# First layer's epilogue: the norm of u from a quadratic form per row, h + y from g and the neighbour sums

## The chip, the cores and the metric

The kernel runs on one core of a Trainium2 chip. The metric is the device time of one execution in microseconds (us). Before the change its median over eight runs is 2209.0 us (2207.34 to 2211.43).

A core has five engines with instruction queues of their own: PE (TensorE, matrix products), DVE (VectorE), ACT (ScalarE), POOL (GpSimd) and SP (SyncE, which here only issues transfers). Each queue is worked off in order; between queues there are semaphores. A tile has 128 partitions.

## What is computed

The reference is four graph layers over 4096 nodes with 128 features and a dense 0/1 adjacency matrix of 4096 x 4096, each followed by a residual sum and a layer norm. Only the first layer matters here. It works in hyperbolic space (c = 1), row by row after one sum over neighbours:

```python
h = proj(mobius_add(proj(mobius_matvec(weight, x)), hyp_bias))
x_tangent = logmap0(h)
x_local = jax.vmap(lambda xi: logmap(xi, h))(h)              # all pairs of rows
adj_att = adj * jax.nn.sigmoid(logits)
support_t = jnp.einsum('ij,ijd->id', adj_att, x_local)       # u, one row per node
h_agg = proj(expmap(h, support_t))                           # tanh(lambda |u| / 2) u / |u|, then mobius_add with h
out = proj(expmap0(proj_tan0(h_agg)))
x = layernorm(x + out)
```

`expmap(h, u)` needs |u| per row, then the Moebius sum of h and a multiple of u, then the norm of that sum; the outer maps need one more norm. So the rows are run over several times, with a few operations on one number per row between the passes.

## The kernel before

All features are float32 in SBUF as 32 row tiles of 128 rows by 128 features, `NT = 32`; a *column* is a 128 x 32 tile that holds one number per row.

The first part of `layer0` builds g = h / (1 - |h|^2) in `H` (the first 128 columns of `HA`), its transpose `HT`, its squared norms `gg`, and columns such as `b`, `bhalf` (b/2), `b2x` (2b), `rb`. Then `pair_loop` runs over the 36 pairs of blocks of 512 rows in an order written out by hand (`PAIR_ORDER`, under a manual schedule). For each pair PE turns the adjacency blocks and forms dot products, ACT and DVE make the weights, and PE sums g over the neighbours (`sum_i` L675, `sum_j` L690); DVE adds the sums up in `XA` (`add_up`, L704). `X` is its first 128 columns: v, the weighted sum of g over the neighbours; its last column is the same sum over the extra column of `HA`.

Behind that stands the epilogue, which is not hand-ordered: the framework's scheduler sets the order of each queue by itself, and buffers come from pools with a fixed count.

- L453 loads x once more into the memory of `HT` (`x0`), a transfer on SP's queue.
- L459: POOL writes `Hb` = b * g, 32 tiles.
- L462 and L465: for each tile DVE takes the dot product of g and v (`gv`), and ACT scales v by b/2 in place.
- L466 to L468: the column `sm`.
- `combine` (L470 to L481) is called in three loops. It puts `src * a + add` into `X` on DVE (L475, one operation per tile) and takes the sum of its squares, on DVE (L477) for some tiles and on ACT (L481) for the others. On both engines such a sum is two instructions: the operation and the read of the accumulator. The calls are
  - L485: u = sm * g + (b/2) v, with |u|^2 into `uu`;
  - L492: w = sg * u + Hb, with |w|^2 into `wsq`;
  - L508: c2 * w + c1 * Hb, with its square into `gsq`.
- Between the first two calls `un` (L488, a square root) and `th` (a tanh) are made on ACT, each with a load of its function table (L239), and `sg` on DVE. Between the last two, `den`, `rden`, `c2`, `c1` (L493 to L501), and then L504 and L506 scale `Hb` by `c1`, odd tiles on POOL, even ones on ACT.
- The rest makes `gf` from `gsq`, and L520 forms x0 + gf * w tile by tile, followed by the layer norm of four tiles at a time (`normalise_tile`).

The second layer begins with transposes of `X` on PE, products with its weights, and transfers of the results (`qk`).

Of the kernel before, what the change touches and what calls it, by code (L numbers as in the profile page):

```python
# [9 lines left out]
F32 = mybir.dt.float32  # L10
F32R = mybir.dt.float32r
AF = mybir.ActivationFunctionType
ALU = mybir.AluOpType
# [3 lines left out]
P = 128  # L17
EPS_LN = 1e-5
MIN_NORM = 1e-15
# [23 lines left out]
class Net:  # L43
# [234 lines left out]
    def layer0(self, x, weight, bias, att_w, att_b):  # L278
        nc, tc, N, NT, D = self.nc, self.tc, self.N, self.NT, self.D
        W1 = min(1024, N)  # L280
        WH = min(1024, N)
        X = self.X
        with ExitStack() as ctx:
# [12 lines left out]
            H = HA[:, :, 0:D]  # L296
# [14 lines left out]
            junk = self.wide.tile([P, 4, P], F32, tag="wt", name="wt")  # L311
# [90 lines left out]
            b = self.ts("b", hsq, -1.0, ALU.mult, 1.0, ALU.add)  # L402
            nc.vector.tensor_scalar(b, b, MIN_NORM, None, op0=ALU.max)
            rb = self.rec("rb", b)
            ga, gb = self.tt("ga", ca, rb, ALU.mult), self.tt("gb", cb, rb, ALU.mult)
            de = self.cols.tile([P, 2, NT], F32, tag="de", name="de")
            gg = self.col("gg")
            for g in self.groups():
                p = self.ps_t.tile([P, 4, P], F32, tag="pt", name="pt")
                for k, t in enumerate(g):  # L410
                    c = slice(t, t + 1)
                    junk = pre.tile([P, P], F32, tag="junk", name="junk", bufs=4)
# [28 lines left out]
            b2x, bhalf = self.ts("b2x", b, 2.0, ALU.mult), self.ts("bhalf", b, 0.5, ALU.mult)  # L441
# [7 lines left out]
            self.pair_loop(HT, HA, dr, ex, rows, adp, early)  # L449


            x0 = HT.rearrange("p (t d) -> p t d", d=D)
            nc.sync.dma_start(out=x0, in_=self.rows(x))  # L453
            late = ctx.enter_context(tc.tile_pool(name="late0", bufs=1))
            rot = ctx.enter_context(tc.tile_pool(name="rot0", bufs=4))
            Hb = late.tile([P, NT, D], F32, tag="Hb", name="Hb")
            gv = self.col("gv")
            for t in range(NT):
                nc.gpsimd.tensor_scalar(Hb[:, t, :], H[:, t, :], b[:, t : t + 1], None, op0=ALU.mult)  # L459
            for t in range(NT):  # L460
                junk = rot.tile([P, P], F32, tag="junk", name="junk")
                nc.vector.scalar_tensor_tensor(  # L462
                    junk, H[:, t, :], 1.0, X[:, t, :], op0=ALU.mult, op1=ALU.mult, accum_out=gv[:, t : t + 1]
                )
                nc.scalar.activation(X[:, t, :], X[:, t, :], AF.Copy, scale=bhalf[:, t : t + 1])  # L465
            sm = self.tt("sm", gv, b2x, ALU.mult)  # L466
            nc.vector.tensor_tensor(sm, sm, self.XA[:, :, D], ALU.subtract)
            nc.vector.tensor_tensor(sm, sm, bhalf, ALU.mult)  # L468

            def combine(t, a, src, add, sq, of_eight):  # L470

                k = slice(t, t + 1)
                junk = rot.tile([P, P], F32, tag="junk", name="junk")
                x = X[:, t, :]
                nc.vector.scalar_tensor_tensor(x, src[:, t, :], a[:, k], add[:, t, :], op0=ALU.mult, op1=ALU.add)  # L475
                if t * of_eight % 8 < of_eight:
                    nc.vector.scalar_tensor_tensor(  # L477
                        junk, x, 1.0, x, op0=ALU.mult, op1=ALU.mult, accum_out=sq[:, k]
                    )
                else:  # L480
                    nc.scalar.activation(junk, x, AF.Square, accum_out=sq[:, k])  # L481

            uu, wsq, gsq = self.col("uu"), self.col("wsq"), self.col("gsq")
            for t in range(NT):
                combine(t, sm, H, X, uu, 2)  # L485


            un = self.norm("un", uu)  # L488
            th = self.act("sg", self.tt("unb", un, rb, ALU.mult), AF.Tanh)
            sg = self.tt("sgu", th, self.rec("run", un), ALU.mult)  # L490
            for t in range(NT):
                combine(t, sg, X, Hb, wsq, 2)  # L492
            den = self.ts("den2", th, -1.0, ALU.mult, 1.0, ALU.add)  # L493
            nc.vector.tensor_scalar(th, th, 1.0, None, op0=ALU.add)
            nc.vector.tensor_tensor(den, den, th, ALU.mult)
# [3 lines left out]
            rden = self.rec("rden2", den)  # L499
            c2 = self.tt("c2", rden, b, ALU.mult)  # L500
            c1 = self.tt("c1", rden, wsq, ALU.mult)  # L501
            for t in range(NT):
                if t % 2:
                    nc.gpsimd.tensor_scalar(Hb[:, t, :], Hb[:, t, :], c1[:, t : t + 1], None, op0=ALU.mult)  # L504
                else:
                    nc.scalar.activation(Hb[:, t, :], Hb[:, t, :], AF.Copy, scale=c1[:, t : t + 1])  # L506
            for t in range(NT):
                combine(t, c2, X, Hb, gsq, 3)  # L508

            gn = self.norm("gn", gsq)  # L510
            gf = self.to_ball("gp", gn)
            gn = self.tt("gn2", gn, gf, ALU.mult)
            nc.vector.tensor_scalar(gn, gn, MIN_NORM, None, op0=ALU.max)
            th = self.act("gth", gn, AF.Tanh)
# [3 lines left out]
            nc.vector.tensor_tensor(gf, gf, self.to_ball("gp2", th), ALU.mult)  # L518
            for t in range(NT):
                nc.vector.scalar_tensor_tensor(  # L520
                    X[:, t, :], X[:, t, :], gf[:, t : t + 1], x0[:, t, :], op0=ALU.mult, op1=ALU.add
                )
                if t % 4 == 3:
                    self.normalise_tile(t // 4, on_scalar=True)
# [1029 lines left out]
```

## Time and profile before

| what | value |
|---|---|
| median of 8 runs | 2209.0 us |
| lowest, highest | 2207.34, 2211.43 us |
| the profiled execution's own time | 2209.21 us |
| its span, first to last instruction | 2207.3 us |
| PE, DVE, ACT, POOL busy in the span | 88%, 85%, 67%, 4% |
| last neighbour sum on PE ends (start of the epilogue) | 766.5 us after the span's start |
| first tile of the last loop (L520) starts | 819.9 us |
| granted PE clock, mean | 0.953 of full speed |

How to read it: the profile gives, for each engine, when an instruction started and how long it was in the engine. Two instructions that follow each other on an engine overlap a little, so the distance of their starts is shorter than the duration of one. A "group" is all instructions of one line and shape, with their mean duration and the idle time of the engine just ahead of them; "<-" names what ended that idle time. The chain of waits is the sequence of work that ended last, followed back from the end of the span.

### The profile page before, as it was taken

To read this page: it belongs to the slowest core of one execution; us is meant where nothing else is said; L and a number is where in the kernel's file an instruction comes from. 1 tells how busy PE (TensorE), PEld (TensorE's weight loads), DVE (VectorE), ACT (ScalarE), POOL (GpSimd) and SP (SyncE) were. 2 spreads that over 40 slices of the span, in tenths; PEclk is the share of its full clock that TensorE was granted. 3 is DMA by queue.
4 is the path that set the end of the run, shared out by engine and by line. 5 is a ranking of instruction groups with operands and counts; after the bars stand their busy time and mean duration, and the time that the engine had idled before them with its cause. 6 is when DMAs were issued, how large, how long until landed. Compare 5 with 4: busy or idle time off the path is not lost.

```text
span 2207.3 us, 24053 instructions
## 1 busy us (share of the span) xinstructions
PE 1945.0 (88%) x8720; PEld 1050.4 (48%) x8720; DVE 1880.9 (85%) x2732; ACT 1476.5 (67%) x1858; POOL 98.1 (4%) x146
## 2 busy tenths in 40 slices
PE   4588888888888708999999999999997999989998
PEld 4376667676666505433333333333333444434443
DVE  6799999999999887789999999999898345458887
ACT  5799999999999774687777787877883212210000
POOL 2000000000000322210000000000000000000000
PEclk7789999999999956999999999999999999999999
DMA  3467565667666307885646465565455777667883
GB/s 93 139 207 242 201 220 203 239 210 244 209 210 213 116 1 247 212 228 173 200 163 188 172 200 180 174 191 175 168 195 229 284 280 272 253 224 270 292 299 111
DMA packets 112868, 448.44 MB, mean 203 GB/s; under 512 B 9760, under 2 KB 20064, under 8 KB 71776
## 3 DMA queue, kind: packets, MB, share of 16 engines
q1 hardware_dynamic: 94160, 361.82, 46.7%
q10 hardware_dynamic: 9360, 68.16, 9.1%
q0 software_dynamic: 9216, 16.78, 4.2%
q8 instruction: 73, 1.20, 0.2%
q14 instruction: 59, 0.48, 0.1%
HBM read 369.10 MB, written 77.63 MB: 202 GB/s over the span
## 4 chain that ended last, share of the span: by engine, by line
PE 40%; DVE 33%; ACT 19%; issue 5%; DMA 3%; SPq 0%; POOL 0%; ACTq 0%; DVEq 0%; POOLq 0%
PE pv L926 10%; PE pa L1260 10%; PE pa L1437 9%; DVE e L909 9%; PE ps L900 6%; ACT e L907 4%; ACT w L612 3%; DVE w L620 3%; DVE nat L890 2%; DVE t L603 2%; DVE t L648 2%; DMA adjT<-at 2%; DVE w L652 2%; ACT at L584 2%; ACT y L627 2%
## 5 line engine op out<-in xcount | busy, mean ns | idle before, releaser
L909 DVE SCALAR_TENSOR_TENSOR e<-at,e 128x2048 f32<-128x2048 f32 x256 | 583.1, 2288 | 69.5 <-ACT e L907 68.9
L907 ACT ACTIVATE e<-ps 128x1024 f32<-128x1024 f32 x512 | 493.6, 1025 | 145.4 <-PE ps L900 125.6
L926 PE MATMUL pv<-e,VA 128*64 128x512 f32 x2048 | 495.8, 605 | 6.9 <-DVE e L909 6.3
L900 PE MATMUL ps<-QS,KS 128*128 128x512 f32 x1024 | 312.7, 424 | 5.3 <-ACT e L907 3.0
L900 PEld LDWEIGHTS ps<-QS,KS 128*128 128x128 f32 x1024 | 171.5, 189 | 230.4 <-ACT e L907 175.3
L926 PEld LDWEIGHTS pv<-e,VA 128*64 128x64 f32 x2048 | 124.7, 136 | 248.8 <-issue 214.6
L1260 PE MATMUL pa<-ring,Y 128*128 128x512 f32 x512 | 227.1, 597 | 0.0
L580 PE MATMUL ptA<-ident,ad 128*128 128x128 f32 x1024 | 158.8, 283 | 59.4 <-ACT at L584 49.5
L1437 PE MATMUL pa<-w,F 128*128 128x512 f32 x448 | 197.0, 598 | 0.0
L580 PEld LDWEIGHTS ptA<-ident,ad 128*128 128x128 f32 x1024 | 120.5, 144 | 139.7 <-ACT at L584 95.3
L1434 DVE SCALAR_TENSOR_TENSOR w<-rho,col,ring 128x512 f32<-128x512 f32 x224 | 162.9, 749 | 25.6 <-PE pa L1437 13.3
L596 PE MATMUL pz<-HT 128*128 128x512 f32 x288 | 154.5, 640 | 21.3 <-DVE w L663 14.2
L675 PE MATMUL pi<-HA,w 128*128 128x129 f32 x1152 | 156.2, 281 | 0.6 <-DVE w L652 0.6
L1260 PEld LDWEIGHTS pa<-ring,Y 128*128 128x128 f32 x512 | 96.7, 193 | 112.8 <-issue 111.9
L620 DVE TENSOR_TENSOR w<-w,at 128x2048 f32<-128x2048 f32 x64 | 146.4, 2287 | 0.5 <-ACT at L584 0.5
L675 PEld LDWEIGHTS pi<-HA,w 128*128 128x128 f32 x1152 | 143.9, 197 | 3.6 <-issue 2.3
L1437 PEld LDWEIGHTS pa<-w,F 128*128 128x128 f32 x448 | 84.3, 191 | 107.2 <-issue 80.0
L881 ACT ACTIVATE nat<-nat 128x2048 f32<-128x2048 f32 x64 | 122.6, 1916 | 4.0 <-DMA nat<-in_adj_dram 4.0
L690 PE MATMUL pj<-HA,w 128*128 128x129 f32 x896 | 109.5, 274 | 3.0 <-DVE w L663 3.0
L603 DVE SCALAR_TENSOR_TENSOR t<-ei,de,pz 128x512 f32<-128x512 f32 x144 | 104.1, 745 | 6.7 <-DMA ei<-rows 6.6
L690 PEld LDWEIGHTS pj<-HA,w 128*128 128x128 f32 x896 | 104.6, 191 | 3.2 <-DVE w L663 3.2
L658 PE MATMUL ptz<-ident,t 128*128 128x128 f32 x448 | 69.0, 281 | 30.0 <-DVE w L663 22.5
(359 smaller groups left out, 2461.8 us busy)
## 6 DMA issues: line engine op xcount, KB each, us to landing
ring<-adjT SPq DMA_DIRECT2D x128, 1024.0 KB, 5.4
ad<-in_adj_dram SPq DMA_DIRECT2D x64, 1024.0 KB, 5.4
adjT<-at SPq DMA_DIRECT2D x64, 1024.0 KB, 4.9
nat<-in_adj_dram ACTq DMA_DIRECT2D x64, 1024.0 KB, 5.0
at<-adjT SPq DMA_DIRECT2D x63, 1024.0 KB, 4.8
qk<-cut SPq DMA_DIRECT2D x16, 512.0 KB, 11.8
KS<-qk POOLq DMA_DIRECT2D x32, 256.0 KB, 7.5
QS<-qk POOLq DMA_DIRECT2D x32, 256.0 KB, 5.8
```

What stands on the lines that cost most here:

```text
L580: nc.tensor.transpose(pt[:, ib, :], ad[:, ib, jb * P : (jb + 1) * P], self.ident)
L596: nc.tensor.matmul(pz, lhsT=HT[:, j * P : (j + 1) * P], rhs=HT[:, I * S : (I + 1) * S], start=True, stop=True)
L620: nc.vector.tensor_tensor(w, w, st[p][f"at{k}"], ALU.mult)
L675: nc.tensor.matmul(row[I, "po"][ib // 2][:, ib % 2, :], lhsT=st[p]["w0"][:, jb, ib * P : (ib + 1) * P], rhs=HA[:, 4 * J + jb, :], start=False,
L690: nc.tensor.matmul(pj[:, a, :], lhsT=st[p]["w1"][:, ib, jb * P : (jb + 1) * P], rhs=HA[:, 4 * I + ib, :], start=(ib == 0), stop=(ib == 3),)
L900: nc.tensor.matmul(p[:, h, :], lhsT=KS[:, h2 + h, jb * P : (jb + 1) * P], rhs=QS[I % 2][:, h2 + h, :], start=True, stop=True,)
L907: nc.scalar.activation(e[:, h2 : h2 + 2, :], p, AF.Exp)
L909: nc.vector.scalar_tensor_tensor(e, at[:, jb % 4, :].unsqueeze(1).to_broadcast([P, NH, S]), 0.0, e, op0=ALU.not_equal, op1=ALU.mult,)
L926: nc.tensor.matmul(st["po"][h // 2][g : g + 64, :], lhsT=VA[:, o : o + 64], rhs=e[:, h, :], start=(jb == 0), stop=(jb == NT - 1), skip_gro ...
L1260: nc.tensor.matmul(st["pa"], lhsT=Y[:, 4 * J + jb, :], rhs=at[:, jb, :], start=False, stop=(J == NS - 1 and jb == 3), skip_group_check=True,)
L1434: nc.vector.scalar_tensor_tensor(w, rho[:, I * S : (I + 1) * S], col[:, 0, j : j + 1], at[:, jb, :], op0=ALU.max, op1=ALU.mult)
L1437: nc.tensor.matmul(pa, lhsT=F[:, j, :], rhs=w, start=False, stop=(j == NT - 1), skip_group_check=True)
```

## The change

u is no longer formed. With u = sm * g + (b/2) v its squared norm is sm^2 |g|^2 + 2 sm (b/2) g.v + (b/2)^2 |v|^2, so the first loop takes |v|^2 (`vv`, on ACT) instead of scaling v, and `quadratic` works on columns alone. `Hb` goes too: w is formed as wg * g + wv * v with wg = sg * sm + b and wv = sg * b/2, and the last combination as c2 * w + (c1 * b) g. For each of these two, `scaled` puts the second product into a buffer `part` (tiles 1, 4 and 6 of every eight on POOL, the others on ACT), and DVE adds the first. The results are kept in a tile of their own, `w`, and the pool of rotating buffers has 6 of each kind instead of 4. Three of four squares are on ACT in both loops. In the changed file the dot product is L480, the square of v L484, `scaled` L473 and L475, the combinations L499 and L523, the squares L502, L506, L526 and L530.

```diff
--- before.py
+++ after.py
@@ -449,47 +449,61 @@
             self.pair_loop(HT, HA, dr, ex, rows, adp, early)
 
 
+
             x0 = HT.rearrange("p (t d) -> p t d", d=D)
             nc.sync.dma_start(out=x0, in_=self.rows(x))
             late = ctx.enter_context(tc.tile_pool(name="late0", bufs=1))
-            rot = ctx.enter_context(tc.tile_pool(name="rot0", bufs=4))
-            Hb = late.tile([P, NT, D], F32, tag="Hb", name="Hb")
-            gv = self.col("gv")
+            rot = ctx.enter_context(tc.tile_pool(name="rot0", bufs=6))
+            w = late.tile([P, NT, D], F32, tag="w", name="w")
+            gv, vv, wsq = self.col("gv"), self.col("vv"), self.col("wsq")
+
+            def quadratic(name, a, c):
+
+                q, r = self.tt(name, a, gg, ALU.mult), self.tt(name + "r", c, gv, ALU.mult)
+                nc.vector.scalar_tensor_tensor(q, r, 2.0, q, op0=ALU.mult, op1=ALU.add)
+                nc.vector.tensor_tensor(q, q, a, ALU.mult)
+                nc.vector.tensor_tensor(r, c, c, ALU.mult)
+                nc.vector.tensor_tensor(r, r, vv, ALU.mult)
+                nc.vector.tensor_tensor(q, q, r, ALU.add)
+                nc.vector.tensor_scalar(q, q, MIN_NORM * MIN_NORM, None, op0=ALU.max)
+                return q
+
+            def scaled(t, dst, src, factor):
+                if t % 8 in (1, 4, 6):
+                    nc.gpsimd.tensor_scalar(dst, src, factor, None, op0=ALU.mult)
+                else:
+                    nc.scalar.activation(dst, src, AF.Copy, scale=factor)
+
             for t in range(NT):
-                nc.gpsimd.tensor_scalar(Hb[:, t, :], H[:, t, :], b[:, t : t + 1], None, op0=ALU.mult)
-            for t in range(NT):
+                k = slice(t, t + 1)
                 junk = rot.tile([P, P], F32, tag="junk", name="junk")
                 nc.vector.scalar_tensor_tensor(
-                    junk, H[:, t, :], 1.0, X[:, t, :], op0=ALU.mult, op1=ALU.mult, accum_out=gv[:, t : t + 1]
+                    junk, H[:, t, :], 1.0, X[:, t, :], op0=ALU.mult, op1=ALU.mult, accum_out=gv[:, k]
                 )
-                nc.scalar.activation(X[:, t, :], X[:, t, :], AF.Copy, scale=bhalf[:, t : t + 1])
+                junk = rot.tile([P, P], F32, tag="junk", name="junk")
+                nc.scalar.activation(junk, X[:, t, :], AF.Square, accum_out=vv[:, k])
             sm = self.tt("sm", gv, b2x, ALU.mult)
             nc.vector.tensor_tensor(sm, sm, self.XA[:, :, D], ALU.subtract)
             nc.vector.tensor_tensor(sm, sm, bhalf, ALU.mult)
 
-            def combine(t, a, src, add, sq, of_eight):
-
-                k = slice(t, t + 1)
-                junk = rot.tile([P, P], F32, tag="junk", name="junk")
-                x = X[:, t, :]
-                nc.vector.scalar_tensor_tensor(x, src[:, t, :], a[:, k], add[:, t, :], op0=ALU.mult, op1=ALU.add)
-                if t * of_eight % 8 < of_eight:
-                    nc.vector.scalar_tensor_tensor(
-                        junk, x, 1.0, x, op0=ALU.mult, op1=ALU.mult, accum_out=sq[:, k]
-                    )
-                else:
-                    nc.scalar.activation(junk, x, AF.Square, accum_out=sq[:, k])
-
-            uu, wsq, gsq = self.col("uu"), self.col("wsq"), self.col("gsq")
-            for t in range(NT):
-                combine(t, sm, H, X, uu, 2)
-
-
-            un = self.norm("un", uu)
+
+            un = self.norm("un", quadratic("uu", sm, bhalf))
             th = self.act("sg", self.tt("unb", un, rb, ALU.mult), AF.Tanh)
             sg = self.tt("sgu", th, self.rec("run", un), ALU.mult)
+            wg, wv = self.tt("wg", sg, sm, ALU.mult), self.tt("wv", sg, bhalf, ALU.mult)
+            nc.vector.tensor_tensor(wg, wg, b, ALU.add)
             for t in range(NT):
-                combine(t, sg, X, Hb, wsq, 2)
+                k = slice(t, t + 1)
+                part = rot.tile([P, P], F32, tag="part", name="part")
+                scaled(t, part, X[:, t, :], wv[:, k])
+                nc.vector.scalar_tensor_tensor(w[:, t, :], H[:, t, :], wg[:, k], part, op0=ALU.mult, op1=ALU.add)
+                junk = rot.tile([P, P], F32, tag="junk", name="junk")
+                if t % 4 == 3:
+                    nc.vector.scalar_tensor_tensor(
+                        junk, w[:, t, :], 1.0, w[:, t, :], op0=ALU.mult, op1=ALU.mult, accum_out=wsq[:, k]
+                    )
+                else:
+                    nc.scalar.activation(junk, w[:, t, :], AF.Square, accum_out=wsq[:, k])
             den = self.ts("den2", th, -1.0, ALU.mult, 1.0, ALU.add)
             nc.vector.tensor_scalar(th, th, 1.0, None, op0=ALU.add)
             nc.vector.tensor_tensor(den, den, th, ALU.mult)
@@ -499,13 +513,21 @@
             rden = self.rec("rden2", den)
             c2 = self.tt("c2", rden, b, ALU.mult)
             c1 = self.tt("c1", rden, wsq, ALU.mult)
+            nc.vector.tensor_tensor(c1, c1, b, ALU.mult)
+
+            gsq = self.col("gsq")
             for t in range(NT):
-                if t % 2:
-                    nc.gpsimd.tensor_scalar(Hb[:, t, :], Hb[:, t, :], c1[:, t : t + 1], None, op0=ALU.mult)
+                k = slice(t, t + 1)
+                part = rot.tile([P, P], F32, tag="part", name="part")
+                scaled(t, part, H[:, t, :], c1[:, k])
+                nc.vector.scalar_tensor_tensor(w[:, t, :], w[:, t, :], c2[:, k], part, op0=ALU.mult, op1=ALU.add)
+                junk = rot.tile([P, P], F32, tag="junk", name="junk")
+                if t % 4 == 3:
+                    nc.vector.scalar_tensor_tensor(
+                        junk, w[:, t, :], 1.0, w[:, t, :], op0=ALU.mult, op1=ALU.mult, accum_out=gsq[:, k]
+                    )
                 else:
-                    nc.scalar.activation(Hb[:, t, :], Hb[:, t, :], AF.Copy, scale=c1[:, t : t + 1])
-            for t in range(NT):
-                combine(t, c2, X, Hb, gsq, 3)
+                    nc.scalar.activation(junk, w[:, t, :], AF.Square, accum_out=gsq[:, k])
 
             gn = self.norm("gn", gsq)
             gf = self.to_ball("gp", gn)
@@ -518,7 +540,7 @@
             nc.vector.tensor_tensor(gf, gf, self.to_ball("gp2", th), ALU.mult)
             for t in range(NT):
                 nc.vector.scalar_tensor_tensor(
-                    X[:, t, :], X[:, t, :], gf[:, t : t + 1], x0[:, t, :], op0=ALU.mult, op1=ALU.add
+                    X[:, t, :], w[:, t, :], gf[:, t : t + 1], x0[:, t, :], op0=ALU.mult, op1=ALU.add
                 )
                 if t % 4 == 3:
                     self.normalise_tile(t // 4, on_scalar=True)
```

## The prediction

> **What bounds the kernel now.** The change touches only the epilogue of the first layer, so I first cut the span into stages (busy time of each engine in each stretch). The page's overall shares (PE 88%, DVE 85%) say nothing here: in these 50 us PE does nothing.
>
> ```profile
> core 0: us, PE busy (x) PEld busy (x) DVE busy (x) ACT busy (x) POOL busy (x), PEclk, DMA share, GB/s
> ...
> 767.20:775.90 8.70, 0.00 (x0) 0.00 (x0) 8.48 (x69) 8.36 (x29) 8.70 (x13) 0.61 0.00 1
> 775.90:786.70 10.80, 0.00 (x0) 0.00 (x0) 10.25 (x48) 9.18 (x53) 1.18 (x7) 0.50 0.00 0
> 786.70:790.10 3.40, 0.00 (x0) 0.00 (x0) 0.94 (x6) 3.02 (x4) 0.00 (x0) 0.50 0.01 2
> 790.10:800.90 10.80, 0.00 (x0) 0.00 (x0) 10.65 (x51) 8.81 (x48) 0.00 (x0) 0.50 0.00 0
> 800.90:802.10 1.20, 0.00 (x0) 0.00 (x0) 1.02 (x5) 0.00 (x0) 0.00 (x0) 0.50 0.00 0
> 802.10:815.40 13.30, 0.00 (x0) 0.00 (x0) 12.32 (x56) 11.32 (x56) 10.64 (x16) 0.50 0.00 1
> ```
>
> The reader sees no PE work and no transfers (last column 0 to 2 GB/s): nothing but DVE, ACT and POOL passing 32 row tiles to each other, with a barrier of small column operations between loops. I name the loops A (767.2, g·v and scaling of X), B (775.9, u and |u|²), C (790.1, w and |w|²) and D (802.1, scaling of Hb, then the combination and its norm). Whatever is saved in one is saved in the span, because the next barrier waits for the last tile. The chain of waits confirms it: it stays in these loops, and the table loads and column operations stand between them.
>
> ```profile
> 786.69 1.28 ACT L239
> 787.99 0.23 ACT un L239
> 788.24 1.28 ACT L239
> 789.53 0.24 ACT sg L239
> 789.79 0.20 DVE sgu L226
> ```
>
> Second, the prices: groups by line with shapes apart, whose mean is a latency, and the timeline, whose start-to-start distance is what a loop pays.
>
> ```profile
> L481 ACT ACTIVATE junk<-X 128x128 f32<-128x128 f32 x68 | 20.5, 304 | 5.8 <-DVE junk L477 2.1 <-DVE X L475 2.1
> L504 POOL TENSOR_SCALAR Hb<-Hb,c 128x128 f32<-128x128 f32 x16 | 10.6, 683 | 25.0 <-DVE c L226 25.0
> L475 DVE SCALAR_TENSOR_TENSOR X<-X,c,Hb 128x128 f32<-128x128 f32 x32 | 10.3, 379 | 0.8 <-POOL Hb L504 0.8
> L475 DVE SCALAR_TENSOR_TENSOR X<-X,sgu,Hb 128x128 f32<-128x128 f32 x32 | 9.3, 360 | 0.0
> ```
>
> ```profile
> 767.54 9.50 ACT L465 ACTIVATE X<-X,bhalf 128x128 f32<-128x128 f32 x32 [12.68 <-DVE junk L462]
> ...
> 778.23 0.29 ACT L481 ACTIVATE junk<-X 128x128 f32<-128x128 f32 x1
> 778.43 0.19 ACT L481 ACTIVATION_READ_ACCUMULATOR junk<-X 128x1 f32 x1
> 778.53 0.30 ACT L481 ACTIVATE junk<-X 128x128 f32<-128x128 f32 x1
> ```
>
> On ACT a square with its accumulator read starts 0.293 us after the one before (778.23 to 778.53; the run from 778.23 on repeats 0.29 to 0.30), and a scaling 9.50/32 = 0.297. So any ACT tile operation costs 0.295, not the 0.30 + 0.19 or 0.40 of the records. On DVE a combination costs 0.264 (four in 1.05 in the chain) and a square 0.21; beside POOL, in loop D, sixteen combinations take 5.18, 0.32 each. A POOL scaling costs 10.64/16 = 0.665. A column operation that depends on the one before starts 0.23 after it, an independent one 0.11.
>
> **What the Trainium skill says.** "ScalarE: Activation LUTs", What ACT_TABLE_LOAD costs, gives 186 ns + 0.833 ns per element, 93 ns more for each pointer operand, and an overlap of 93 ns back to back: at 128 elements 293 ns, and 386 with a pointer scale. The trace agrees (304 and 402 ns records, 0.293 and 0.297 apart), so a pointer scale is free in a row. The table load it gives, 1283 ns, is the 1.28 above. "SBUF — State Buffer", SBUF: two separate sides, says that a DVE operation with two SBUF inputs and a GpSimd operation that reads SBUF lock each other out of a shared port for a whole instruction. Loop D agrees only weakly: POOL works without a pause, and DVE still does a combination every 0.32 instead of 0.264. I take the measured 0.32.
>
> **The change, part by part.** Who waits for whom in the built program, against the measured prices:
>
> *POOL's Hb (32 scalings, 752.4 to 776.7) goes.* It gains nothing itself: its reader is loop C, at 790. The small memsets of hd behind it on POOL just come earlier.
>
> *Loop A.* The ACT scaling of X becomes a square with sum (vv); the same 32 at 0.293 instead of 0.297. The first square no longer waits for DVE's g·v, but for the last PE matmul (766.5): the first four run from 766.55. The fifth needs the buffer of DVE's third g·v (about 768.0, the dot products still start at 767.2 behind the last sum). From there ACT sets the pace: 768.05 + 28 × 0.293 = 776.25. DVE's last g·v waits for a buffer from four squares before and ends at 775.6.
>
> *Loop B goes*: 32 combinations and 8 squares on DVE, 24 squares on ACT. In its place eight column operations on DVE join the three of sm. From 775.68: sm in three steps of 0.23 to 0.37 (776.53), five dependent steps and one independent one to the maximum, its end at 777.95. The square root's table load on ACT needs no input, and runs beside it from 776.25 to 777.53. So un starts at 778.0 instead of 787.99: **10.0 us saved**. un to sgu stays 1.80.
>
> *Between sgu and loop C* wg, wv are formed first: the scalings start 0.58 after sgu where the first combination started 0.29 after it.
>
> *Loop C.* Before, DVE bound it (32 × 0.264 + 8 × 0.21 = 10.1). Now each tile first needs part = wv·v, 20 on ACT and 12 on POOL, then the combination on DVE, then the square, 24 on ACT and 8 on DVE. ACT has 44 × 0.295 = 13.0; DVE the 10.1, or 11.9 at 0.32; POOL 12 × 0.665 = 8.0. ACT binds. Its order is two or three parts, then two to four squares: the first square waits for the first combination, which stands behind POOL's first part (0.665) and one more combination on DVE, so it starts at about 1.3 where the three parts took 0.9: 0.4 lost. After that every combination is due at least 0.2 before its square. With the last accumulator read 13.5. From sgu to the sum with wsq: 0.58 + 13.5 = 14.1 instead of 800.92 - 789.79 = 11.1. **3.0 lost.**
>
> *Column operations before loop D*: one more product (c1·b) in front of the scalings, **0.2 lost**.
>
> *Loop D* has the same 44, 12 and 32 + 8: 13.5 to the next table load, against 815.43 - 802.13 = 13.3, in which 16 scalings on POOL and the order of ACT (16 scalings, then 20 squares) set the time. **0.2 lost.**
>
> *The last loop* reads w instead of X, same count and shape: 0. The x0 load is issued behind the same PE matmul, and transfers are quiet from 755 to 820, so it isn't late. Everything behind the epilogue (transposes, qk, first attention block) hangs on the last row tile and moves with it; nothing there has a clock of its own in the chain.
>
> Sum: 10.0 - 3.0 - 0.2 - 0.2 = 6.6, of which I take 6.5. The profiled execution took 2209.2 (span 2207.3 and 1.9 around it), the median is 2209.0: **2202.5**. ACT's own work grows from 116 to 120 tile operations; the gain is the barrier-to-barrier time of a loop on which DVE had 44 operations that now fall away.
>
> What the trace does not show is the alternation itself: ACT, DVE and ACT again within a tile. From below it costs nothing beyond the 0.4 (ACT's own 13.0 can't shrink, so the gain is 7.4 at most). From above, if each of the eight batches per loop paid the 0.42 of the first, 3.0 more per loop, the gain would be 0.5. I take near the lower end, since the waits are met 0.2 to 0.6 early by the sums above.
>
> **The rivals.** *Hand-offs.* ACT's parts and squares wait in turn for DVE. For it: margins of only 0.2 in places, and DVE slower beside POOL. Against: six buffers, and DVE has 1.1 to 2.9 us to spare per loop. With half the batches paying: 3 us given back, 2205.5; with all, 2208.5.
>
> *The gain is taken up behind the epilogue*: 2209. For it only that PE's clock stands at 0.50 here and must rise again; against it the chain, which runs through the epilogue without slack.
>
> *POOL becomes the bound* (the other side: slower). A POOL part that waits for the port while DVE combines delays its own tile, and DVE in order waits for it, and ACT's squares behind. For it: one scaling of Hb took 2.52 us, beside DVE's long operations, and Hb<-Hb,c reached 0.79. Against: DVE's operations here are ten times shorter. POOL passes ACT from 13.5/12 = 1.1 us per part; the 6.6 are gone when each loop takes 3.3 more, 16.8/12 = 1.4 us. At 1.6 us a loop takes 19.2 + 0.3, 12 more in both: 2214.5.
>
> **How the numbers follow.** Chances: as summed 0.65, hand-offs 0.2, nothing left 0.07, POOL 0.08. A measurement of this kernel tells 0.2% (4.4 us) from no change, so faster needs 2204.6 or less: all of the first, a third of the second: 0.72. Same 0.20. Slower 0.08. The range goes from 2200.5 (the 7.4, and 1 us of the runs' own spread, 2207.3 to 2211.4) to 2207.5, into the hand-offs.
>
> **What would show it.** In the changed profile: no loop with DVE combining into X before un; un some 10 us earlier after the last sums; ACT busy without idle (over 12.5 of 13.5) in loops C and D, DVE idle before its combinations for ACT's parts; the two loops 13 to 14 long each. I am wrong if ACT shows idle time of more than 2 us in a loop waiting for DVE (hand-offs), if POOL's parts last over 1.1 us, or if the epilogue is shorter and the span is not.

## The result, and the profile after

The changed kernel takes 2200.15 us (median of 11 runs, 2198.3 to 2205.39) where the kernel before takes 2208.96 in the same comparison (31 runs); the ratio is 0.9967, 95% interval 0.9958 to 0.9975. So it is faster, by 0.42% to 0.25%, and 2.4 us below the time predicted; the median stands 0.35 us under the lower end of the range given, 2200.5, and the mean of the same runs, 2201.5, inside it. Its profiled execution took 2201.9, with a span of 2200.2.

The epilogue, from the end of PE's last sum to the first tile of the last loop, goes from 53.4 us (766.51 to 819.90) to 47.9 (763.87 to 811.76). It is cut below at the barriers of the changed kernel: the squared norm of v and the dot products, the table loads of un and sg, loop C, the columns, loop D, the columns of gf. Busy time of each engine in each stretch, kernel after:

```profile
core 0: us, PE busy (x) PEld busy (x) DVE busy (x) ACT busy (x) POOL busy (x), PEclk, DMA share, GB/s
763.90:775.10 11.20, 0.00 (x0) 0.00 (x0) 10.77 (x77) 10.93 (x66) 0.47 (x5) 0.66 0.00 1
775.10:776.90 1.80, 0.00 (x0) 0.00 (x0) 0.68 (x4) 1.70 (x3) 0.00 (x0) 0.50 0.00 0
776.90:791.50 14.60, 0.00 (x0) 0.00 (x0) 13.07 (x56) 13.37 (x68) 7.60 (x12) 0.50 0.00 1
791.50:792.90 1.40, 0.00 (x0) 0.00 (x0) 1.21 (x6) 0.01 (x1) 0.00 (x0) 0.50 0.00 0
792.90:807.30 14.40, 0.00 (x0) 0.00 (x0) 12.21 (x48) 13.36 (x69) 7.57 (x12) 0.50 0.00 1
807.30:811.80 4.50, 0.00 (x0) 0.00 (x0) 2.62 (x13) 4.29 (x5) 0.00 (x0) 0.50 0.00 0
```

Loop B has no stretch any more: un follows the first pass after columns only. In loops C and D the busiest engine is now ACT (13.37 of 14.60 and 13.36 of 14.40); in C before, DVE was (10.65 of 10.80). POOL, which did nothing in C, now has 7.60.

Where ACT is not working shows in the chain of waits, kernel after (start, duration, engine, what, line):

```profile
775.05 0.23 ACT un L239
...
776.86 0.19 DVE sgu L226
...
777.58 0.61 POOL part L473
...
778.21 0.73 DVE w L499 x2
...
778.97 0.65 ACT junk L506 x4
...
790.06 0.30 ACT part L475
...
790.39 0.36 DVE w L499
...
790.77 0.70 ACT junk L506 x4
...
792.90 0.48 issue
793.39 0.61 POOL part L473
```

At the start of C the chain goes POOL, DVE, ACT: ACT's first square (778.97) waits for two combinations, and both of them stand behind POOL's first part, which ends at 778.19. Then the chain stays on ACT from 778.97 to 790.36, and at the end the last tile goes ACT, DVE, ACT once more. Loop D begins the same way, but POOL starts its first part only at 793.39, after 0.48 of "issue".

The groups by line with shapes apart, cut to the epilogue of the kernel after, say the same (busy us, mean ns, idle time just ahead and what ended it):

```profile
L499 DVE SCALAR_TENSOR_TENSOR w<-HA,wg,part 128x128 f32<-128x128 f32 x32 | 10.5, 374 | 1.3 <-ACT part L475 0.7 <-POOL part L473 0.5
L473 POOL TENSOR_SCALAR part<-HA,c 128x128 f32<-128x128 f32 x12 | 7.6, 633 | 8.2 <-DVE c L516 4.5 <-DVE w L523 3.7
L506 ACT ACTIVATE junk<-w 128x128 f32<-128x128 f32 x24 | 7.1, 298 | 0.7 <-DVE w L499 0.6
L530 ACT ACTIVATE junk<-w 128x128 f32<-128x128 f32 x24 | 7.1, 298 | 1.0 <-DVE w L523 0.9
```

ACT's squares waited for DVE 0.6 us in C and 0.9 in D; DVE's combinations in C waited 1.3 us in all; a POOL part takes 0.63. The prediction would have been wrong at 2 us of ACT's waiting or at 1.1 us for a POOL part, and neither is near. One sign of its own it missed: the loops were to be 13 to 14 us long each, and from the first part to the barrier they take 14.1 and 14.4.

### The profile page after: what moved, and what is told of

It reads as the page before. It is cut to its first block, busy times and chain, and to the rows that moved or that the text cites. A ratio compares the mean times of both kernels' runs of the same rounds, so it can differ in the third digit from the quotient of the medians.

```text
span 2200.2 us, 23952 instructions
## 1 busy us (share of the span) xinstructions
PE 1948.3 (89%) x8720; PEld 1053.5 (48%) x8720; DVE 1873.9 (85%) x2688; ACT 1474.7 (67%) x1874; POOL 78.6 (4%) x122
## 4 chain that ended last, share of the span: by engine, by line
PE 40%; DVE 31%; ACT 22%; issue 5%; DMA 2%; POOL 0%; SPq 0%; ACTq 0%; DVEq 0%; POOLq 0%
PE pv L948 10%; PE pa L1282 10%; PE pa L1459 9%; DVE e L931 9%; PE ps L922 6%; ACT w L634 4%; ACT e L929 4%; DVE w L642 3%; DVE nat L912 2%; DVE t L625 2%; ACT at L606 2%; DVE w L674 2%; DVE t L670 2%; ACT y L652 2%; ACT t L666 2%
```

## The experiments

All edits are to the changed kernel. The table holds the stages of every profiled execution, in us, from the starts in the timelines; the medians are those of the kernel's own timed runs. The kernel before had medians of 2208.53 to 2208.96 in the four comparisons.

| kernel | PE's end to un | un to sgu | sgu to den | den to table load | to the last loop | epilogue | median (runs) |
|---|---|---|---|---|---|---|---|
| before | 21.48 | 1.80 | 11.13 | 14.51 | 4.47 | 53.39 | 2208.96 (31) |
| before again | 21.62 | 1.80 | 11.13 | 14.51 | 4.47 | 53.53 | 2207.77 (12) |
| after | 11.18 | 1.81 | 14.64 | 15.78 | 4.48 | 47.89 | 2200.15 (11) |
| after again | 11.15 | 1.81 | 14.60 | 15.76 | 4.47 | 47.79 | 2200.23 (5) |
| u formed again | 20.43 | 1.80 | 14.27 | 15.76 | 4.47 | 56.73 | 2211.60 (21) |
| Hb kept | 11.65 | 1.81 | 21.02 | 15.38 | 4.47 | 54.33 | 2208.90 (13) |
| loop D as before | 11.64 | 1.81 | 21.03 | 14.47 | 4.47 | 53.42 | 2209.25 (13) |
| Hb in place | 11.73 | 1.81 | 14.59 | 15.38 | 4.47 | 47.98 | 2199.89 (5) |
| loop D as before, Hb in place | 11.40 | 1.80 | 14.59 | 14.47 | 4.47 | 46.73 | 2201.84 (8) |
| 4 buffers | 11.75 | 1.80 | 15.22 | 16.38 | 4.47 | 49.62 | 2199.46 (5) |
| 12 squares on DVE | 11.15 | 1.81 | 13.60 | 14.64 | 4.47 | 45.67 | 2199.59 (5) |
| the same, other parts on POOL, 4 squares of v on DVE | 10.69 | 1.81 | 13.94 | 15.23 | 4.47 | 46.14 | 2199.19 (6) |
| 12 squares on DVE, 4 squares of v on DVE | 10.68 | 1.80 | 13.57 | 14.57 | 4.47 | 45.09 | 2198.99 (5) |
| delay in the chain | 16.34 | 1.80 | 14.61 | 15.75 | 4.47 | 52.97 | 2207.55 (21) |

**u formed again.** Loops A and B of the kernel before stand ahead of loops C and D of the changed one, with the factors sg and b in C where wv and wg are.

```diff
-                nc.scalar.activation(junk, X[:, t, :], AF.Square, accum_out=vv[:, k])
+                nc.scalar.activation(X[:, t, :], X[:, t, :], AF.Copy, scale=bhalf[:, k])
...
-            un = self.norm("un", quadratic("uu", sm, bhalf))
+            for t in range(NT):
+                nc.vector.scalar_tensor_tensor(X[:, t, :], H[:, t, :], sm[:, k], X[:, t, :], op0=ALU.mult, op1=ALU.add)
+                ...
+            un = self.norm("un", uu)
```

> Undoes the quadratic form alone: u is formed again in loop B (32 combinations on DVE, its squares 8 on DVE and 24 on ACT) and the first loop scales v again; loops C and D and the missing Hb stay as in the changed kernel. Theory (the gain is the removed loop B, the parts cost time in C and D): from the last sum on PE to un 21.5 us less what the slower POOL-loaded dot products cost, so 20.5 to 21.5, against 11.2 in the changed kernel and 21.5 in the kernel before; loops C and D as long as in the changed kernel, 14.6 from sgu and 14.4. Whole kernel about 10 us slower than the changed one, 4 to 5 slower than the one before: 2210 to 2214. Rival (the gain came from POOL's Hb disappearing beside PE's last sums, not from the quadratic form): this kernel keeps the gain, 2200 to 2203.

2211.6 us, ratio to the kernel before 1.0014 (1.0007 to 1.002). Busy time by stretch, this kernel:

```profile
765.40:785.80 20.40, 0.00 (x0) 0.00 (x0) 18.35 (x117) 18.55 (x81) 0.47 (x5) 0.55 0.00 0
```

PE's end to un is 20.4 us, against 11.2 in the changed kernel and 21.5 before, and the parts cost what they cost in the changed kernel (15.76 in D, and in C 14.27, where wg and wv are not formed). The pass that forms u is worth 9.25 us of the 10.3 in this stage (20.43 against 11.18), and C and D alone are a loss. Hb is absent here too, so its absence is not the main gain. It does have a part in it: this kernel comes to its first combination 8.39 us after PE's end, the kernel before 9.38, since its dot products, without POOL beside them, take 6.9 us and not 7.8.

**Hb kept**, its 32 scalings back on POOL, and read by nobody.

```diff
             w = late.tile([P, NT, D], F32, tag="w", name="w")
+            Hb = late.tile([P, NT, D], F32, tag="Hb", name="Hb")
+            for t in range(NT):
+                nc.gpsimd.tensor_scalar(Hb[:, t, :], H[:, t, :], b[:, t : t + 1], None, op0=ALU.mult)
```

> The changed kernel with POOL's 32 scalings of Hb put back at their old place, 24 us beside the end of the pair loop and the first loop; nothing reads them. Theory (Hb only cost idle time of POOL): the epilogue is 47.9 us from the last sum to the first x0 + gf * w as in the changed kernel, at most 0.5 more since the dot products run beside POOL; whole kernel within 1.5 us of the changed one. Rival (POOL's load is what slowed PE's last 32 sums, 5.48 us before and 3.84 after, through its granted clock): those sums take 5 us or more again, and the kernel is 2 to 3 us slower than the changed one.

2208.9 us, ratio 1.0001 (0.9993 to 1.0009): a miss for every theory, since the edit did another thing than meant. The chain of waits, this kernel (POOL's part is L476 here):

```profile
765.60 12.85 POOL Hb L460 x21
...
778.97 6.39 POOL Hb L460 x11
...
786.04 0.62 POOL part L476
```

Behind w, Hb's scalings waited for PE's last sums (POOL sat idle until `pi`, L700) and started at 765.60 instead of 752.4; that Hb's memory there is what these sums still used is inferred from the wait. They ran until 785.4, and the first part of loop C, due some 0.6 us after sgu (778.89), stood behind them in POOL's queue until 786.04. The epilogue is 6.4 us longer. Work that nobody reads was on the path through the order of its engine's queue.

**Hb in place**: the same scalings, with Hb and w in pools of their own, so that Hb's memory is free as early as before.

```diff
             rot = ctx.enter_context(tc.tile_pool(name="rot0", bufs=6))
-            w = late.tile([P, NT, D], F32, tag="w", name="w")
+            latew = ctx.enter_context(tc.tile_pool(name="late1", bufs=1))
+            w = latew.tile([P, NT, D], F32, tag="w", name="w")
+            Hb = late.tile([P, NT, D], F32, tag="Hb", name="Hb")
...
```

> The changed kernel with POOL's 32 scalings Hb = b*H back, not read by anything, now in a pool of their own so that their memory is free as early as it was in the kernel before (w's pool is placed after the rotating buffers). Theory: they run at about 752 to 777 us beside the pair loop and the first pass, as before, POOL is free when the first part is due, and the epilogue is 47.9 to 48.5 us; 2199.5 to 2202. Then the 6.4 us that the same scalings cost in the run with their memory released late were only their place in POOL's queue. Rival: dropping Hb is worth 1 to 3 us by itself, since POOL's work beside the pair loop slows DVE's last sg work or the sums: the sums take 5.4 us and the epilogue starts 1 to 2.7 us later; 2201.5 to 2204.

2199.89 us, ratio 0.9964 (0.9951 to 0.9976), epilogue 47.98. All instructions of the tile Hb, this kernel:

```profile
L461 POOL TENSOR_SCALAR Hb<-HA,b x32: 594/606/2537, 751.9 to 774.7; 128x128 f32<-128x128 f32 x32
```

At the old place Hb costs 0.1 us of epilogue, the sum of two parts that nearly cancel: 0.55 more ahead of un, where POOL works beside the columns (sm at L491 takes 0.31 instead of 0.20 in the chain), and 0.40 less in D. So the removal of Hb is worth nothing in sum, as it was costed, and the 6.4 us of the run above are its place in the queue. PE's end stands at 762.21 in this run, the earliest of all profiles, so POOL's work beside the pair loop doesn't make the epilogue start late.

**Loop D as before**, Hb kept at the late place. The product c1 * b goes too, and 12 of the 32 squares are on DVE, as in the kernel before.

```diff
-            nc.vector.tensor_tensor(c1, c1, b, ALU.mult)
...
-                scaled(t, part, H[:, t, :], c1[:, k])
-                nc.vector.scalar_tensor_tensor(w[:, t, :], w[:, t, :], c2[:, k], part, op0=ALU.mult, op1=ALU.add)
+                if t % 2:
+                    nc.gpsimd.tensor_scalar(Hb[:, t, :], Hb[:, t, :], c1[:, t : t + 1], None, op0=ALU.mult)
+                else:
+                    nc.scalar.activation(Hb[:, t, :], Hb[:, t, :], AF.Copy, scale=c1[:, t : t + 1])
+            for t in range(NT):
+                nc.vector.scalar_tensor_tensor(w[:, t, :], w[:, t, :], c2[:, k], Hb[:, t, :], op0=ALU.mult, op1=ALU.add)
...
```

> The changed kernel with only the last combination undone: Hb = b * g on POOL, scaled by c1 half on POOL and half on ACT, then c2 * w + Hb, as before. Theory (ACT with 44 operations sets loop D at 14.4 us, the old loop at 13.3): loop D 13.3, epilogue 1.1 + 0.2 shorter than the changed kernel's, whole kernel about 1.3 faster than the changed one, if Hb's 24 us on POOL are free. Rival (the loop is set by its two barriers and not by ACT's count): loop D stays at 14.4, no difference.

2209.25 us, ratio 0.9998 (0.999 to 1.0007): the time expected was missed and says nothing of loop D, since Hb delayed loop C as above. The stage itself is 14.47 against 15.38 in the run with Hb kept. The run was repeated with Hb in place:

> Loop D of the kernel before (32 scalings of Hb by c1, 16 on POOL and 16 on ACT, then 32 sums, 12 of the 32 squares on DVE) in the changed kernel, Hb's 32 scalings in the place and time that they had before. Now POOL is free when the loops start. Theory: ACT has 36 operations in D in the place of 44 and D is set by DVE: den to table load 14.4 to 14.8 us against 15.4 in the run with Hb in place and the changed loop D, epilogue 47.0 to 47.4; time 0.5 to 1.5 below that run's, 2198.5 to 2200.5. Rival: with POOL not delayed D's old form has no advantage (the new form's first part starts earlier too), epilogue 47.9 to 48.3; 2200 to 2202.

The stage is 14.47 again, against 15.38 in the run with Hb in place and the new D, and the epilogue 46.73, the shortest of those with 8 squares on DVE in C (0.33 of it from an earlier un). The time doesn't follow: 2201.84 us, ratio 0.9971 (0.996 to 0.9981), above the expectation. The means of 8 and 5 runs (2201.9 and 2200.1) have standard errors of 0.6 each, so a microsecond can't be read from them. Groups of loop D, this kernel:

```profile
L529 DVE SCALAR_TENSOR_TENSOR w<-w,c,Hb 128x128 f32<-128x128 f32 x32 | 10.3, 377 | 0.7 <-POOL Hb L523 0.7
L535 ACT ACTIVATE junk<-w 128x128 f32<-128x128 f32 x20 | 5.9, 298 | 2.0 <-DVE junk L531 1.1 <-DVE w L529 0.6
```

In the old D it is ACT that waits for DVE (2.0 us) and DVE hardly waits (0.7): the two forms of D are bound by different engines. The chain of the kernel before says the same, with DVE on it from 802.86 to 813.98; two of its pieces:

```profile
802.86 1.09 DVE X L475 x3
...
804.16 4.37 DVE X L475 x14
```

**Four buffers** of part and junk instead of six.

```diff
-            rot = ctx.enter_context(tc.tile_pool(name="rot0", bufs=6))
+            rot = ctx.enter_context(tc.tile_pool(name="rot0", bufs=4))
```

> The changed kernel with 4 rotating buffers in the place of 6 for part and junk. Theory (ACT's 44 operations of 0.30 us set loops C and D, the hand-offs only the entry and the end): POOL's part of tile t then waits for w of tile t-4; ACT keeps its queue order, some 0.2 to 1 us is added to each of C and D, and the sgu to den and den to table load stretches read 14.6 to 15.6 and 15.8 to 16.8 us; 2200 to 2203. Rival (the hand-offs between POOL, DVE and ACT bind, and buffers are what hides them): C and D are 2 us or more longer each, ACT shows idle time of over 1 us per loop before its squares; 2204 to 2208.

2199.46 us, ratio 0.996 (0.9947 to 0.9973). C and D are 0.6 us longer each, and so is the first pass; ACT's squares waited 1.0 and 1.4 us instead of 0.7 and 1.0. The lengths of C and D are what the theory gave; the time is 0.5 below its range. Six buffers do not hide a large hand-off cost: with fewer, each loop pays 0.6, not 3. But the bound changed: from the first part of C at 776.85 to 788.6 the chain of waits has no piece on ACT any more, only POOL's parts and DVE's operations in turn, with a part waiting for a buffer and the next combination for the part. With four buffers it is the hand-offs that bind, as the rival had it, at 0.6 us per loop in place of its 2 or more.

**12 squares on DVE** in each of C and D, 20 on ACT.

```diff
-                if t % 4 == 3:
+                if t % 8 in (2, 5, 7):
```

> The changed kernel with 12 instead of 8 of the 32 squares on DVE in loops C and D: ACT has 40 operations instead of 44 in each, DVE 4 more. Theory (ACT's 44 x 0.295 bind and DVE has room): 4 x 0.295 = 1.2 less on ACT, DVE's 32 x 0.31 + 12 x 0.22 = 12.6 comes close, so each loop 0.6 to 1.2 shorter; whole kernel 1.2 to 2.4 faster than the changed one. Rival (hand-offs between the engines set the loop): no change or longer, since each square on DVE delays the combination behind it.

2199.59 us, ratio 0.9956 (0.9942 to 0.9969). C is 1.04 and D 1.14 us shorter. Four ACT operations at 0.293 are 1.17: each operation taken from ACT came off the loop nearly whole, which is how ACT is known to bind in the changed kernel. The median is only 0.6 below the changed kernel's where 1.2 to 2.4 were expected; five runs don't tell these apart. In this version ACT is the bound no longer: from its first combination (776.56) to the barrier the chain of waits in C has only DVE. The last two of this series change the rest of ACT's share. First 4 of 32 squares of v go to DVE in loop A, and POOL gets parts 2, 4 and 7 of each eight:

```diff
-                if t % 8 in (1, 4, 6):
+                if t % 8 in (2, 4, 7):
                     nc.gpsimd.tensor_scalar(dst, src, factor, None, op0=ALU.mult)
...
+                if t % 8 == 5:
+                    nc.vector.scalar_tensor_tensor(
+                        junk, X[:, t, :], 1.0, X[:, t, :], op0=ALU.mult, op1=ALU.mult, accum_out=vv[:, k]
+                    )
+                else:
                     nc.scalar.activation(junk, X[:, t, :], AF.Square, accum_out=vv[:, k])
```

> The run with 12 squares on DVE in loops C and D, and in addition: 4 of the 32 squares of v in the first pass on DVE, and POOL's parts at tiles 2, 4 and 7 of each eight in the place of 1, 4 and 6, so that ACT makes the first two parts and its first square waits for a part of its own. Theory (ACT's count of operations sets each of the three loops, and the entry stall is POOL's first part of 0.61 us against ACT's 0.30): PE's end to un becomes 10.0 to 10.9 us from 11.2, the entry stall falls from 0.57 and 0.90 to 0.2 to 0.4 us, sgu to den reads 13.0 to 13.5, den to table load 14.0 to 14.5; epilogue 44 to 45 us; 2197 to 2199.5. Rival: DVE's chain binds at the end of the first pass (it has 4 more operations of 0.29 us there) and the order of parts does nothing; then un is not earlier and the epilogue is 45.5 to 46 us, as in the run before; 2199 to 2200.5.

2199.19 us, ratio 0.9957 (0.9943 to 0.9971). un is 0.46 earlier, inside the range, but C and D became 0.34 and 0.59 longer instead of shorter: a miss on the order of parts. The chains show where in C: with the first two parts now ACT's, DVE starts its combinations 0.31 us sooner after sgu, as meant, but takes 0.28 longer over them, and the barrier comes 0.46 after its last combination instead of 0.09, because a square on ACT (792.56) stands last there. In D the start was not sooner (0.14 later), and the end costs 0.38 more in the same way. The next run takes the order back and keeps the rest:

> The run with 12 squares on DVE, POOL's parts where the changed kernel has them (tiles 1, 4, 6 of each eight), and 4 of the 32 squares of v in the first pass on DVE; the order of the parts of the run before this is taken back. Theory: the order of the parts was what made sgu to den and den to table load 0.3 and 0.6 us longer there, since POOL's parts met DVE's squares; they read 13.5 to 13.7 and 14.5 to 14.8 us again, PE's end to un reads 10.6 to 10.8, epilogue 45.0 to 45.5; 2198 to 2200. Rival: those 0.3 and 0.6 were scatter or came from elsewhere, and they stay; epilogue 46 or more; 2198.5 to 2200.5.

2198.99 us, ratio 0.9959 (0.9945 to 0.9973), epilogue 45.09, the shortest: C and D are back at 13.57 and 14.57, so the order of the parts was the loss. Busy time by stretch, this kernel (loops C and D):

```profile
777.50:791.10 13.60, 0.00 (x0) 0.00 (x0) 12.97 (x65) 12.29 (x60) 8.39 (x12) 0.50 0.00 1
791.10:805.70 14.60, 0.00 (x0) 0.00 (x0) 13.16 (x62) 12.21 (x61) 8.35 (x12) 0.50 0.00 1
```

DVE is the busier, 12.97 of 13.60, and ACT has time to spare: by this table there is nothing to gain from moving more to DVE (not tried). By its stages this is the best version, 2.8 us of epilogue below the changed kernel. Its five runs alone hardly tell the two apart; the three versions with 12 squares on DVE together, 16 runs, have a mean of 2199.0 against the changed kernel's 2201.35, 2.4 less with a standard error of 0.8, where their epilogues are 2.2 shorter.

**Where the rest of the gain is.** The two profiled executions differ by 5.5 us of epilogue and by 2.65 in the end of PE's last sums, ahead of it. The chain of waits has the last 32 sums, kernel before:

```profile
761.09 5.42 PE pi L675 x32
```

and in the changed kernel 3.78 for the same 32. Both kernels were profiled a second time for this.

> The changed kernel as it is, a second profile beside the other variants of this call. Open is why the medians fell by 8.8 us where the two profiled executions show the epilogue shorter by 5.5 us and PE's last sums ending 2.7 us earlier. Theory: the 32 last sums of the pair loop take 3.8 or 5.4 us by the phase of PE's granted clock in that execution and not by the program, so this profile may show either, and the epilogue from PE's end to the first x0 + gf*w is again 47.9 us within 0.3. Rival: the changed program itself gives PE a better clock at the end of the pair loop; then the sums again take 3.8 us and PE ends near 764. Time by both: 2198 to 2202.

> The kernel before, a second profile. Theory (the 32 last sums take 3.8 or 5.4 us by the phase of the granted clock in an execution): they may take either here, PE ends between 762 and 767, and the epilogue from there is 53.4 us within 0.3. Rival (the program decides): again 5.4 us and PE's end at 766 to 767. Time 2207 to 2211.

After again: 3.78 us, PE's end at 766.15, median 2200.23, ratio 0.9965 (0.9952 to 0.9978). Before again, chain of waits:

```profile
763.16 3.78 PE pi L675 x32
```

The kernel before has 3.78 too, its end is at 766.94, and its time is its usual one (2207.77; against the other runs of the same kernel 0.9994, 0.9986 to 1.0003). So the duration of the last sums goes with the execution and not with the program. Over the 14 profiles PE's end lies between 762.2 and 766.9. The granted clock was 0.74 of full in the one stretch of sums (760 to 766.6, first profile of before) and 1.00 in the other (759 to 764, after), which had its low clock just ahead, 0.78 and 0.80 from 751 to 759. PE's busy time and granted clock (the number behind the bracket), before and after:

```profile
760.00:766.60 6.60, 6.49 (x36) 0.74 0.01 2
...
759.00:764.00 5.00, 4.86 (x36) 1.00 0.01 3
```

The two profiles of the kernel before are among the three with the latest end, though, and with two of them it stays open whether that is chance. From the first tile of the last loop to the end of the span it is 1387.4 and 1385.4 us before, 1388.4 and 1385.8 after: nothing is gained there.

Mean times stand further apart than the epilogues: 2208.4 (131 runs of the kernel before) against 2201.3 (16 of the kernel after), 7.0 us with 1.1 to either side, where the epilogues differ by 5.6 (53.46 and 47.84, means of two profiles). In the two pairs of profiles the span falls by 7.1 and 6.2 us, of which 2.6 and 0.8 stand ahead of the epilogue. A delay asks whether a microsecond of epilogue counts for more than one:

```diff
+            uq = quadratic("uu", sm, bhalf)
+            for _ in range(24):
+                nc.vector.tensor_scalar(uq, uq, 1.0, None, op0=ALU.mult)
-            un = self.norm("un", quadratic("uu", sm, bhalf))
+            un = self.norm("un", uq)
```

> The changed kernel with 24 DVE multiplications of the 128x32 column uq by 1.0, each on the result of the one before, put between the quadratic form and un: a pure delay of the chain of some 5.5 us (24 by the 0.23 us from one dependent column operation to the next, seen between the additions at 793.71 and 793.94 in the second profile of the changed kernel), with nothing else changed. It asks where the rest of the gain comes from: mean times differ by 7.2 us, epilogues by 5.6. Theory (a microsecond of epilogue is a microsecond of time, and the rest is scatter of the executions): 2206.5 to 2207.5, against 2201.3 mean of the changed kernel's runs. Rival (the length of the epilogue counts 1.2 to 1.3 times, since the work after it also starts at another phase or clock): 2208 to 2209, as the kernel before.

The timeline, this kernel:

```profile
777.02 5.15 DVE L492 TENSOR_SCALAR uu<-uu 128x32 f32<-128x32 f32 x24
782.20 0.23 ACT L239 ACTIVATE un<-uu 128x32 f32<-128x32 f32 x1 [5.30 <-DVE uu L492]
```

The epilogue is 5.1 us longer than the changed kernel's and the mean of 21 runs is 2206.75 (median 2207.55), 5.4 above the changed kernel's, with a standard error of 0.8: one for one as near as this can tell, and below the rival's 2208 to 2209. The ratio to the kernel before is 0.9994 (0.9987 to 1.0). A factor of 1.2, which would be 6.2 us, is one standard error away and not excluded: a straight line through the mean times of the changed kernel and its ten variants rises by 1.12 us per us of epilogue, with a standard error of 0.12. The 1.4 us between 7.0 and 5.6, give or take 1.1, stay open.

## Why the prediction was right

The direction, the mechanism and the bound of the new loops were right; the gain in the epilogue was smaller than summed, 5.5 instead of 6.6, and the time fell further than either, 8.8 by the medians and 7.4 by the means of the same runs. The prediction had 7.4 as the most that could be gained.

- *The chain of small loops bounds the epilogue.* Right: the delay of 5.1 us cost 5.4.
- *Loop A.* Right: the 0.293 per square and the end of the pass were as given. PE's end to un is 11.18 in place of 21.48, **10.3 saved where 10.0 was summed**. Un to sgu stayed.
- *Loop C* was put at 3.0 lost and cost 3.5. ACT binds, as the 12 squares on DVE showed. The term that was too small is what stands around the 44 operations: first part to den (14.64 less the 0.55 from sgu to that part) takes 14.09 where 13.5 was summed. The entry cost 0.57, not 0.4, and there is an exit, not in the sum at all: after ACT's last part (790.06) the last combination starts 0.33 later, the last square 0.38 after that, and ACT has nothing else to do, 0.41 idle. Both starts come 0.02 to 0.03 after the end of the record before, so the lone last tile pays whole records, while in a row the operations overlap.
- *The column product* cost 0.17, put at 0.2.
- *Loop D* was put at 0.2 lost and cost 1.1: **the worst-sized term, and the step that failed**. It counted 13.5 for the new form, by the same sum as C. It has the entry at 0.90, since POOL starts its first part 0.51 us after ACT's (0.16 in C), and the exit of 0.41; 14.40 in all. The old form, put back, takes 14.47 from den to the table load where the new one takes 15.38, with the late Hb and with Hb in place. Of these 0.9 us 0.2 are the column product, and 0.7 the loop itself, with 44 operations on ACT instead of 36; the old form has DVE as its bound, where the prediction named POOL's scalings and the order of ACT. The other 0.4 is POOL's later start.
- *Hb's removal at nothing*: right in the old place (0.1 us), but by luck: 0.55 ahead of un and 0.40 in D, neither of them in the sum, nearly cancel. And POOL is on the path of the changed kernel, and Hb would have had to be out of its queue by then.
- *Hand-offs as rival.* Not what happened: one wait of ACT at the entry of each loop, and the exit; no batch between pays it. With four buffers the hand-offs do bind, and 0.6 per loop is given back.
- *POOL as bound.* Not what happened: 0.63 us per part where 1.1 would have passed ACT. That DVE and POOL shut each other out of a shared port for a whole instruction, as the Trainium skill has it ("SBUF — State Buffer", SBUF: two separate sides), shows as little as in the old loop D. In loop C with 12 squares and 4 squares of v on DVE, one at a time, POOL's 12 parts at 0.592 (the shortest there) and DVE's 32 combinations at 0.264 and 12 squares at 0.21 would need some 18 us, an estimate from these durations, and the loop takes 13.60; a POOL part takes 0.70 there.
- *The gain taken up behind the epilogue.* Not what happened: what follows the epilogue keeps its length within its scatter, 1384.1 to 1388.4 us in the 14 profiles.
- *Two readings that the sum does not use.* Loop B had 40 operations on DVE (32 and 8), not the 44 of the prediction's closing remark. And that a scaling and a square follow each other at the same distance (0.297 and 0.293) does not make the pointer scale free: in the lines shown, the read of the accumulator starts 0.20 after its square (778.23, 778.43) and the next square 0.10 after the read, so the square's distance has the read in it.

The sum of 6.6 became 10.3 - 3.5 - 0.2 - 1.1 = 5.5. With the terms as measured the forecast would have been 2203.5, further from the 2200.15 that came. What the time moved beyond the epilogue is not explained by the prediction's terms, and that it lies on the other side of their error is luck.

## What to carry to other kernels

Where three engines pass small tiles to each other between barriers, count each engine's operations by their start-to-start distance and take the largest, then add the hand-offs at the entry and at the exit of each loop at full record length: the first and last tile have nothing beside them. Before work is added to an engine that was idle, look at what already stands in its queue and at which memory that waits for; and to judge a change of a few microseconds read the stages in two profiles of each kernel, since the stage ahead of it here ended up to 4.7 us apart over the 14 profiles, and 2.3 apart in the two of the changed kernel.

## What the runs showed of the hardware

- POOL's first part of D started 0.50 to 0.51 us after ACT's, released by the same column, in all eight profiles that have the new D and no Hb, and 0.13 after it in the two with Hb (kept and in place), whose 32 more instructions stand earlier in POOL's queue. The profile calls it "issue"; its cause was not tried. It accounts for nearly all of the 0.40 us by which D is shorter there.
- POOL's scaling of 128x128 takes 0.63 us on average where DVE is busy 13.07 of 14.60 us (changed kernel, C) and 0.70 where it is busy 12.97 of 13.60 (12 squares and 4 squares of v on DVE), but 0.70 too with four buffers, where it is busy 13.14 of 15.20. So DVE's share of the time alone does not set it.
- 24 dependent operations on a 128x32 column took 5.15 us on DVE, 0.215 each.
